# Where layer 1's two biases are added: bfloat16 products on TensorE, or adds on GpSimd and VectorE

## The chip, the cores and the metric

The kernel runs on one core of a Trainium2 chip. The metric is device time in microseconds (us). Before the change the median of three runs is 1116.52 us (1116.37 to 1117.14). One further execution was taken with the hardware profiler: it took 1114.53 us, of which 1112.8 us lie between its first and its last instruction (the span).

Five engines work beside each other, each through its own queue in order: PE (TensorE, matrix products and transposes; PEld is its weight load), DVE (VectorE), ACT (ScalarE), POOL (GpSimd) and SP (SyncE, which here issues the DMAs). POOL cannot read PSUM, the memory that PE writes to; DVE and ACT can.

## The reference, cut to what matters

Four graph layers run over x, 32 batches of 512 nodes with 128 features. Each layer normalises x, takes the positive part, applies its own function and adds the result to x. The change is in layer 1 alone:

```python
h = relu(layernorm(x))
# layer 1
h = h @ Wp + bp                               # 512 x 128
scores = h @ a_src [:, None] + h @ a_dst [None, :]
attn = softmax(where(adj <= 0, lowest, leaky(scores, 0.2)))
h_gat = relu(layernorm((attn * adj) @ h) * gat_g + gat_b)
h_gin = (1 + eps) * h_gat + adj @ h_gat
z = h_gin @ W1 + b1
z = relu(layernorm(z) * mlp_g + mlp_b)        # the inner norm
x = x + relu(z @ W2 + b2 + h_gat)
```

`bp` and `b1` are the two biases of the title. Both stand ahead of a layer norm over the features, so only their deviation from their own mean matters for the features: the kernel works with centred weights and centred biases. `bp` also moves the two scores of a node, by `bp . a_src` and `bp . a_dst`.

## The kernel before, in words

A batch is a tile of 128 partitions x 4 chunks x 128 features (512 nodes, four chunks of 128). All of x stays on the chip in `xs`. Nothing loops at run time: the program is unrolled, one chain of operations for every pair of layer and batch, 32 chains for each of the four layers, and two side chains, `prepare` (weights and biases, beside layer 0) and `prepare_last` (layer 3's attention matrix, beside layer 1).

The order on every engine is written out by a planner (`Plan.run`). Every `op(engine, length, emit, reads, writes)` gives it a length in us and the values that the operation reads and writes. It goes through a model of the five engines and always emits the operation that can begin first, among equals the one with the earliest due time. A chain's due times begin a gap after the chain before it (13.3 for layer 1) and at most 7 chains (`WINDOW`) are open at once. Buffers come from rooms of fixed size: 8 PSUM banks, 5 tiles written by DVE, 6 by ACT, 5 by POOL, 5 for the projected and scored `h`, 9 spare ones. What the planner emits first on an engine runs first there, whether or not it is ready.

Layer 1's chain (L793 to L856), the engine of each step in brackets:

- the outer norm: statistics [DVE L475, L477], negative mean [DVE L501], reciprocal deviation by a power [POOL L487, L489], `xn` [POOL L510, four instructions], transposes to `pt` [PE L386], relu to `hT` [ACT L519]
- the projection (`project_scored`), twice for two chunks each: a product of bfloat16 `ones3` with `b3_p` [PE L552, 128x260] opens the PSUM group, two float32 products [PE L557] add to it; then a copy to `h` [ACT L377]. Columns 0 to 127 are the features, column 128 the source score, column 129 the destination score
- the attention (`attend`): the destination scores are spread over all partitions by transposes to `prow` [PE L386]; `y = prow + mask` with its row maximum [DVE L587, four]; `top` and `nmax` [DVE L598, L602]; leaky relu with the source score as bias [ACT L612, four]; exponential with its sum [ACT L620, four]; transposes [PE L386]; `pT = pt * adjT` [DVE L629, four]; `po = pT' h` [PE L640]
- the norm of the attention's result: `q`, statistics of `po`, `ve` [DVE L802, L475, L806], power [POOL L815], `hn` [DVE L822, four], `+ gat_b` [POOL L827], relu to `hg` [ACT L829]
- `pg = hg' adjTe` [PE L834], copy to `ginT` [ACT L377], `hgb = hg + b2` [POOL L842]
- the inner layer: a product of `ones3` with `b3_1` [PE L530, 128x512] opens the group, then `pz` [PE L535]; statistics of `pz`, read in PSUM [DVE L475, L477]; power [POOL L487, L489]; `zn = pz * rz` [DVE L846]; transposes [PE L386]; `zT` with relu, gain and bias [ACT L850]; `px` [PE L535]; `res` and `xs` [DVE L854, L855]

The bfloat16 operands are made once in `prepare`: the centred bias is split into three bfloat16 terms, which lie in rows 0 to 2 of `b3_p` and `b3_1`, and `ones3` has ones in its first three rows, so that one bfloat16 product adds the bias at float32's precision to every node. The split takes DVE instructions (L972 to L992).

Of the kernel before, what the change touches and what calls it, by code (L numbers as in the profile page):

```python
# [229 lines left out]
def kernel(  # L230
# [52 lines left out]
    def const(name, shape, dtype=F32):  # L283
        return cp.tile(list(shape), dtype, name=name)
# [18 lines left out]
    def value(r, name):  # L303
        return Value(Slot(r, name))
# [50 lines left out]
    b3_p = const("b3_p", (P, P2), BF16)  # L355
    b3_1 = const("b3_1", (P, P), BF16)
    ones3 = const("ones3", (P, P), BF16)
# [8 lines left out]
    v_bias, v_w1, v_w2, v_wz, v_b3, v_adjTe, v_rows, v_mlp = (Value() for _ in range(8))  # L366
# [97 lines left out]
    def dve(length, emit, reads, writes):  # L464
        op(DVE, length, emit, reads, writes)
# [16 lines left out]
    def inv_dev(mv):  # L482
        rstd = Value()

        def emit():
            ve = small("ve")
            nc.gpsimd.tensor_scalar(ve, mv.own[:, :, 1], LN_EPS, 1.0, ALU.add, ALU.mult)  # L487
            rstd.own = small("rstd")
            nc.gpsimd.tensor_tensor(rstd.own, ve, mhalf, ALU.pow)  # L489

        op(POOL, 1.3, emit, [mv], [rstd])
        return rstd
# [29 lines left out]
    def column(hT, c):  # L522
        return hT.t[:, c, :]

    def project(hT, w, reads, b3=None, name="p"):
        pt = value(banks, name)

        def emit():
            if b3 is not None:
                nc.tensor.matmul(  # L530
                    pt.t, lhsT=ones3, rhs=b3.rearrange("p (o f) -> p o f", o=1).to_broadcast([P, C, P]),
                    start=True, stop=False,
                )
            for c in range(C):
                nc.tensor.matmul(  # L535
                    pt.t[:, c, :], lhsT=column(hT, c), rhs=w,
                    start=(b3 is None), stop=(b3 is None or c == C - 1),
                )

        op(PE, 0.9 + (0.22 if b3 is not None else 0.0), emit, [hT, *reads], [pt])  # L540
        return pt

    def project_scored(hT, w_ext, reads, b3=None):

        h = parts(scored, "h", 2)
        for k in range(2):
            pt = value(banks, "proj")

            def emit(k=k, pt=pt):
                p = pt.t.rearrange("p (c t) f -> p c (t f)", c=2)[:, :, 0:P2]  # L550
                if b3 is not None:
                    nc.tensor.matmul(  # L552
                        p, lhsT=ones3, rhs=b3.rearrange("p (o f) -> p o f", o=1).to_broadcast([P, 2, P2]),
                        start=True, stop=False,
                    )
                for c in range(2):
                    nc.tensor.matmul(  # L557
                        p[:, c, :], lhsT=column(hT, 2 * k + c), rhs=w_ext,
                        start=(b3 is None), stop=(b3 is None or c == 1),
                    )  # L560

            op(PE, 0.46 + (0.11 if b3 is not None else 0.0), emit, [hT, *reads], [pt])
            copy_op(
                ACT, 0.26, lambda k=k: h[k].t[:, 2 * k : 2 * k + 2, :],
                lambda pt=pt: pt.t.rearrange("p (c t) f -> p c (t f)", c=2)[:, :, 0:P2], [pt], [h[k]],
            )
        return h
# [7 lines left out]
    def attend(h, weights, v_weights):  # L575
# [19 lines left out]
        def emit_top():  # L595

            ntop.own = small("top")
            nc.vector.scalar_tensor_tensor(ntop.own, rmax.own, -1.0, h[0].t[:, :, P], ALU.mult, ALU.subtract)  # L598
# [5 lines left out]
        dve(0.08, emit_top, [*top, *h], [ntop])  # L604
# [3 lines left out]
        for ib in range(C):  # L608

            def emit_leaky(ib=ib):  # L610
                yw = wide(y[ib].t)
                nc.scalar.activation(yw, yw, AF.Prelu, alpha=0.2, bias=h[0].t[:, ib, P : P + 1])  # L612

            op(ACT, 0.61, emit_leaky, h, [y[ib]])
# [30 lines left out]
            op(PE, 0.9, emit_po, [pT, *h], [po[ib]])  # L645
# [147 lines left out]
    def layer1(b):  # L793
        hT, _ = preln(b)
        h = project_scored(hT, w1_ext, [v_w1, v_b3], b3_p)
        po, ssum = attend(h, adjT, v_adjT)
# [46 lines left out]
        pz = project(ginT, wz, [v_wz, v_b3], b3_1, "pz")  # L843
        rz = inv_dev(variances(lambda c: pz.t[:, c, :], [pz]))
        zn = value(by_dve, "zn")
        op(DVE, 0.6, lambda: nc.vector.tensor_mul(zn.t, pz.t, per_chunk(rz.own)), [pz, rz], [zn])  # L846
# [5 lines left out]
        px = project(zT, wts[:, W_2, :], [v_wts[W_2]], name="px")  # L852
# [6 lines left out]
    def layer2(b):  # L859
        hT, _ = preln(b)  # L860
        h = project_scored(hT, w2_ext, [v_w2])
        po, ssum = attend(h, None, None)
# [19 lines left out]
    def layer3(b):  # L882
# [7 lines left out]
        p1 = project(hT, wts[:, W_31, :], [v_wts[W_31]], name="p1")  # L890
# [21 lines left out]
    def prepare():  # L912
        wt_p, wt_1, wt_l2, row_p, row_1 = (value(spare, n) for n in ("wt_p", "wt_1", "wt_l2", "row_p", "row_1"))
# [13 lines left out]
        load(lambda: row_p.t[:, 0, :], all_rows(l1_bp), [row_p], 0.25)  # L927
        load(lambda: wt_1.t[:, 0, :], l1_w1, [wt_1], 0.25)
        load(lambda: row_1.t[:, 0, :], all_rows(l1_b1), [row_1], 0.25)
# [15 lines left out]
        def centred(dst, src, reads, writes):  # L945
# [8 lines left out]
        bp_c = value(spare, "bp_c")  # L954
        b1_c = value(spare, "b1_c")
        centred(lambda: w1_ext[:, 0:P], lambda: wt_p.t[:, 0, :], [wt_p], [v_w1])
        centred(lambda: wz, lambda: wt_1.t[:, 0, :], [wt_1], [v_wz])
        centred(lambda: wide(bp_c.t)[:, 0:P], lambda: row_p.t[:, 0, :], [row_p], [bp_c])
        centred(lambda: wide(b1_c.t)[:, 0:P], lambda: row_1.t[:, 0, :], [row_1], [b1_c])
# [4 lines left out]
        op(PE, 0.15, lambda: nc.tensor.matmul(  # L964
            pc1.t[:, 0, 0:2], lhsT=bp_rep.t[:, 0, :], rhs=a1[:, 0:2], start=True, stop=True), [bp_rep, v_a1], [pc1])
        copy_op(DVE, 0.1, lambda: wide(bp_c.t)[:, P:P2], lambda: pc1.t[:, 0, 0:2], [pc1], [bp_c])


        not0, not01, sel = (const(n, (P, 1)) for n in ("not0", "not01", "sel"))
        v_sel = Value()  # L970

        def selectors():  # L972
            nc.vector.tensor_scalar(not0, ident[:, 0:1], -1.0, 1.0, ALU.mult, ALU.add)
            nc.vector.tensor_sub(not01, not0, ident[:, 1:2])
            nc.vector.tensor_reduce(sel, ident[:, 0:3], AX.X, ALU.add)
            nc.vector.tensor_copy(ones3, sel.to_broadcast([P, P]))

        dve(0.5, selectors, [], [v_sel, v_b3])
        for src, out3, n in ((bp_c, b3_p, P2), (b1_c, b3_1, P)):
            tmp = value(spare, "terms")  # L980

            def terms(src=src, out3=out3, n=n, tmp=tmp):
                full = wide(src.t)[:, 0:n]
                kept = wide(tmp.t)[:, 0:P].bitcast(BF16)[:, 0:n]
                part = wide(tmp.t)[:, 2 * P : 2 * P + n]
                for drop in (not0, not01):
                    nc.vector.tensor_copy(kept, full)
                    nc.vector.tensor_scalar(part, kept, drop, None, ALU.mult)
                    nc.vector.tensor_sub(full, full, part)
                nc.vector.tensor_copy(out3, full)  # L990

            dve(1.2, terms, [v_sel], [src, tmp, v_b3])  # L992
# [256 lines left out]
```

## Time and profile before

| | busy us, whole span | share | busy us, 207 to 720 us (layer 1) |
|---|---|---|---|
| PE | 1085.5 | 98% | 505.31 of 513 |
| DVE | 922.5 | 83% | 452.25 of 513 |
| ACT | 672.1 | 60% | 316.57 of 513 |
| POOL | 673.2 | 60% | 279.96 of 513 |

The span is 1112.8 us, the profiled execution's own time 1114.53 us, the median of the unprofiled runs 1116.52 us. The granted TensorE clock is 0.994 over the span, 1.00 in every stretch from 40 us to 1080 us.

How to read it: busy is the union of an engine's instructions, each from its start to its end. Matmuls are pipelined, so one of 275 ns is followed by the next after about 110 ns; what a product costs is the distance to the next start, not its length. The stretch from 207 to 720 us begins with the first L552 (207.5 us) and ends with the last `xs` of layer 1 (718.3 us). It also holds the last chains of layer 0, the first of layer 2, and most of `prepare_last`.

### The profile page before, as it was taken

What the parts mean: (1) busy time and instruction counts of PE and PEld (TensorE: products, weight loads), DVE (VectorE), ACT (ScalarE), POOL (GpSimd) and SP (SyncE); (2) the same over time, 40 slices, a digit from 0 to 9 for tenths busy, and PEclk for the clock granted to TensorE, in tenths of its full rate; (3) what the DMA queues carried; (4) which work ended last, traced back from release to release, by engine and by line L of the source; (5) the groups of instructions that cost most, each with busy time, mean ns of one, the idle gap of its engine ahead of it and who ended that gap; (6) DMA issues with size and microseconds to landing.
All of it is one profiled execution on the core that took longest, in us unless ns stands there. A gap on an engine that the chain in (4) does not pass through costs nothing.

```text
span 1112.8 us, 25144 instructions
## 1 busy us (share of the span) xinstructions
PE 1085.5 (98%) x8680; PEld 989.0 (89%) x8683; DVE 922.5 (83%) x3822; ACT 672.1 (60%) x1588; POOL 673.2 (60%) x1040
## 2 busy tenths in 40 slices
PE   5999999999999999999999999899999999999998
PEld 4899999998787877887788887899999999999997
DVE  8989899978889898998989897977777777777772
ACT  3456455567365565574656765866667766766661
POOL 8355454554546555646456555687776777777773
PEclk8899999999999999999999999999999999999999
DMA  7202210000000000000000000000100000000001
GB/s 189 58 11 50 43 36 2 2 2 2 1 1 1 1 1 1 1 1 1 1 1 2 1 1 1 1 20 20 30 21 20 21 20 20 20 21 29 21 21 39
DMA packets 56911, 20.50 MB, mean 18 GB/s; under 512 B 21584, under 2 KB 56272, under 8 KB 56784
## 3 DMA queue, kind: packets, MB, share of 16 engines
q1 hardware_dynamic: 56784, 18.90, 6.9%
q8 instruction: 69, 1.13, 0.4%
q14 instruction: 58, 0.48, 0.1%
HBM read 10.43 MB, written 8.39 MB: 17 GB/s over the span
## 4 chain that ended last, share of the span: by engine, by line
PE 75%; DVE 16%; ACT 3%; POOL 2%; issue 1%; SPq 1%; DMA 1%; POOLq 0%; ACTq 0%; DVEq 0%
PE po L640 16%; PE pt L386 13%; PE po L784 10%; PE po L901 10%; PE proj L557 6%; PE pg L834 5%; DVE y L587 4%; PE prow L386 3%; PE po L776 2%; ACT y L620 2%; DVE st L475 2%; PE po L897 2%; PE p L535 2%; DVE pT L629 2%; PE pz L535 1%
## 5 line engine op out<-in xcount | busy, mean ns | idle before, releaser
L640 PE MATMUL po<-h,pT 128*128 128x128 f32 x2048 | 244.2, 275 | 1.7 <-DVE pT L379 1.0
L510 POOL TENSOR_SCALAR xn<-xs,nmean,rstd 128x128 f32<-128x128 f32 x512 | 232.0, 469 | 19.7 <-DVE st L475 9.6
L640 PEld LDWEIGHTS po<-h,pT 128*128 128x128 f32 x2048 | 236.3, 192 | 5.8 <-issue 1.9
L620 ACT ACTIVATE y<-y,nmax 128x512 f32<-128x512 f32 x256 | 181.7, 712 | 41.1 <-DVE nmean L501 20.1
L612 ACT ACTIVATE y<-y,h 128x512 f32<-128x512 f32 x256 | 165.4, 712 | 37.4 <-DVE rmax L587 37.1
L489 POOL TENSOR_TENSOR rstd<-ve,mhalf 128x4 f32<-128x4 f32 x160 | 163.9, 1024 | 13.4
L587 DVE CUSTOM_DVE_ANT_0 y<-prow,bias 128x512 f32<-128x512 f32 x256 | 161.9, 683 | 9.5 <-PE prow L386 9.0
L519 ACT ACTIVATE hT<-pt 128x512 f32<-128x512 f32 x128 | 75.5, 591 | 125.0 <-PE pt L386 123.2
L386 PE MATMUL pt<-ident,y 128*128 128x128 f32 x1024 | 135.1, 274 | 2.5 <-ACT y L620 1.8
L901 PE MATMUL po<-h,offT 128*128 128x128 f32 x1024 | 135.4, 275 | 0.5 <-ACT h L377 0.5
L487 POOL TENSOR_SCALAR ve<-mv 128x4 f32<-128x4 f32 x160 | 36.7, 229 | 160.9 <-DVE rsum L756 57.7
L386 PEld LDWEIGHTS pt<-ident,y 128*128 128x128 f32 x1024 | 115.7, 141 | 20.0 <-ACT y L620 11.4
L834 PE MATMUL pg<-adjTe,hg 128*128 128x512 f32 x256 | 128.2, 593 | 0.0
L901 PEld LDWEIGHTS po<-h,offT 128*128 128x128 f32 x1024 | 124.6, 192 | 0.6 <-ACT h L377 0.6
L475 DVE BATCH_NORM_STATS2 st<-xs 128x6 f32<-128x128 f32 x512 | 109.9, 276 | 1.5 <-POOL xs L879 1.4
L557 PE MATMUL proj<-w_ext,hT 128*128 128x130 f32 x768 | 107.8, 279 | 2.3 <-ACT hT L519 2.3
L557 PEld LDWEIGHTS proj<-w_ext,hT 128*128 128x128 f32 x768 | 97.7, 194 | 6.7 <-ACT hT L519 2.9
L377 ACT COPY h<-proj 128x260 f32<-128x260 f32 x192 | 67.6, 371 | 46.3 <-PE proj L557 40.5
L879 POOL TENSOR_TENSOR xs<-xs,em 128x512 f32<-128x512 f32 x32 | 40.9, 1278 | 81.2 <-DVE em L878 81.2
L386 PE MATMUL pt<-ident,xn 128*128 128x128 f32 x512 | 85.2, 279 | 2.7 <-POOL xn L510 1.9
L629 DVE TENSOR_TENSOR pT<-pt,adjT 128x512 f32<-128x512 f32 x128 | 82.1, 680 | 3.4 <-PE pt L386 3.2
L742 ACT ACTIVATE y<-y,nmax 128x256 f32<-128x256 f32 x128 | 63.8, 501 | 31.1 <-DVE rs L760 14.0
(189 smaller groups left out, 2101.2 us busy)
## 6 DMA issues: line engine op xcount, KB each, us to landing
xs<-in_x_dram SPq DMA_DIRECT2D x32, 256.0 KB, 3.6
out_dram<-yo SPq DMA_DIRECT2D x32, 256.0 KB, 2.2
u<-h SPq DMA_DIRECT2D x128, 0.5 KB, 1.8
bias<-in_adj_dram SPq DMA_DIRECT2D x4, 256.0 KB, 3.3
wts<-in_L_gnn_W_dram SPq DMA_DIRECT2D x3, 64.0 KB, 3.8
rows<-in_L_gnn_bias_dram SPq DMA_DIRECT2D x2, 64.0 KB, 3.3
wt_o<-L_gnn_others_weight_dram SPq DMA_DIRECT2D x1, 64.0 KB, 2.3
wts<-n_L_gnn_self_weight_dram SPq DMA_DIRECT2D x1, 64.0 KB, 3.8
```

Of the source, the lines that this page charges most:

```text
L386: nc.tensor.transpose(dst(k), src(k), ident)
L475: nc.vector.bn_stats(st[:, c, :], src(c))
L489: nc.gpsimd.tensor_tensor(rstd.own, ve, mhalf, ALU.pow)
L510: nc.gpsimd.tensor_scalar(xn.t[:, c, :], src[:, c, :], nmean.own[:, c : c + 1], rstd.own[:, c : c + 1], ALU.add, ALU.mult,)
L557: nc.tensor.matmul(p[:, c, :], lhsT=column(hT, 2 * k + c), rhs=w_ext, start=(b3 is None), stop=(b3 is None or c == 1),)
L587: nc.vector.tensor_tensor_reduce(wide(y[ib].t), wide(prow.t), bias[:, ib, :], 1.0, LOWEST, ALU.add, ALU.max, rmax.own[:, ib : ib + 1],)
L612: nc.scalar.activation(yw, yw, AF.Prelu, alpha=0.2, bias=h[0].t[:, ib, P : P + 1])
L620: nc.scalar.activation(yw, yw, AF.Exp, bias=nmax.own[:, ib : ib + 1], accum_out=ssum[0].own[:, ib : ib + 1])
L640: nc.tensor.matmul(po[ib].t[:, ib, :], lhsT=pT.t[:, jb, :], rhs=h[0].t[:, jb, 0:P], start=(jb == 0), stop=(jb == C - 1),)
L784: nc.tensor.matmul(po[ib].t[:, ib, :], lhsT=w, rhs=(hs if ib < H else hs2).t[:, jb, :], start=False, stop=(jb == C - 1),)
L834: nc.tensor.matmul(wide(pg.t), lhsT=hg.t[:, nb, :], rhs=adjTe[:, nb, :], start=(nb == 0), stop=(nb == C - 1))
L901: nc.tensor.matmul(po[ib].t[:, ib, :], lhsT=offT[:, jb, blk(ib)], rhs=h1.t[:, jb, :], start=False, stop=(jb == C - 1),)
```

## The change

The two bias products leave TensorE, with `b3_p`, `b3_1`, `ones3` and what made them. In their place:

- `src`, the source score with both score biases in it (`score_p`, one number in every partition), is made by a DVE instruction of 4 columns as soon as `h` is copied; `top` and the leaky relu read it instead of `h`'s column 128. A bias on the destination score and the same on the source score come to the same sum.
- the feature bias is added to `h`'s columns 0 to 127 in place by one POOL instruction, which only the products `po` wait for.
- `b1` is added to `pz` by DVE, from PSUM into `zn`; the statistics are then taken from `zn` in SBUF, and the scaling by `rz`, which was DVE's, is done by ACT in place, one instruction for each chunk.
- in `prepare` the centred biases are left as float32 rows, and one small product more adds the two score biases up.

```diff
-    b3_p = const("b3_p", (P, P2), BF16)
-    b3_1 = const("b3_1", (P, P), BF16)
-    ones3 = const("ones3", (P, P), BF16)
+    row_p = const("row_p", (P, 1, P))
+    row_1 = const("row_1", (P, 1, P))
+    score_p = const("score_p", (P, 1))
...
-    def project(hT, w, reads, b3=None, name="p"):
+    def project(hT, w, reads, name):
...
-            if b3 is not None:
-                nc.tensor.matmul(
-                    pt.t, lhsT=ones3, rhs=b3.rearrange("p (o f) -> p o f", o=1).to_broadcast([P, C, P]),
-                    start=True, stop=False,
-                )
...
-    def project_scored(hT, w_ext, reads, b3=None):
+    def project_scored(hT, w_ext, reads):
...
-                if b3 is not None:
-                    nc.tensor.matmul(
-                        p, lhsT=ones3, rhs=b3.rearrange("p (o f) -> p o f", o=1).to_broadcast([P, 2, P2]),
-                        start=True, stop=False,
-                    )
...
-    def attend(h, weights, v_weights):
+    def attend(h, src, v_src, v_h, weights, v_weights):
...
-            nc.vector.scalar_tensor_tensor(ntop.own, rmax.own, -1.0, h[0].t[:, :, P], ALU.mult, ALU.subtract)
+            nc.vector.scalar_tensor_tensor(ntop.own, rmax.own, -1.0, src(), ALU.mult, ALU.subtract)
...
-                nc.scalar.activation(yw, yw, AF.Prelu, alpha=0.2, bias=h[0].t[:, ib, P : P + 1])
+                nc.scalar.activation(yw, yw, AF.Prelu, alpha=0.2, bias=src()[:, ib : ib + 1])
...
-            op(PE, 0.9, emit_po, [pT, *h], [po[ib]])
+            op(PE, 0.9, emit_po, [pT, *v_h], [po[ib]])
...
-        h = project_scored(hT, w1_ext, [v_w1, v_b3], b3_p)
-        po, ssum = attend(h, adjT, v_adjT)
+        h = project_scored(hT, w1_ext, [v_w1])
+        src, v_h = Value(), Value()
+
+        def emit_src():
+            src.own = small("src")
+            nc.vector.tensor_scalar(src.own, h[0].t[:, :, P], score_p, None, ALU.add)
+
+        dve(0.08, emit_src, [*h, v_score_p], [src])
+        op(POOL, 1.25, lambda: nc.gpsimd.tensor_add(
+            h[0].t[:, :, 0:P], h[0].t[:, :, 0:P], row_p.to_broadcast([P, C, P])), [*h, v_row_p], [v_h])
+        po, ssum = attend(h, lambda: src.own, [src], [v_h], adjT, v_adjT)
...
-        pz = project(ginT, wz, [v_wz, v_b3], b3_1, "pz")
-        rz = inv_dev(variances(lambda c: pz.t[:, c, :], [pz]))
+        pz = project(ginT, wz, [v_wz], "pz")
         zn = value(by_dve, "zn")
-        op(DVE, 0.6, lambda: nc.vector.tensor_mul(zn.t, pz.t, per_chunk(rz.own)), [pz, rz], [zn])
+        op(DVE, 0.6, lambda: nc.vector.tensor_add(zn.t, pz.t, row_1.to_broadcast([P, C, P])), [pz, v_row_1], [zn])
+        rz = inv_dev(variances(lambda c: zn.t[:, c, :], [zn]))
+
+        def emit_zn():
+            for c in range(C):
+                nc.scalar.activation(zn.t[:, c, :], zn.t[:, c, :], AF.Copy, scale=rz.own[:, c : c + 1])
+
+        op(ACT, 0.88, emit_zn, [rz], [zn])
...
-        centred(lambda: wide(bp_c.t)[:, 0:P], lambda: row_p.t[:, 0, :], [row_p], [bp_c])
-        centred(lambda: wide(b1_c.t)[:, 0:P], lambda: row_1.t[:, 0, :], [row_1], [b1_c])
+        centred(lambda: row_p[:, 0, :], lambda: row_p[:, 0, :], [], [v_row_p])
+        centred(lambda: row_1[:, 0, :], lambda: row_1[:, 0, :], [], [v_row_1])
...
-        dve(0.5, selectors, [], [v_sel, v_b3])
-        for src, out3, n in ((bp_c, b3_p, P2), (b1_c, b3_1, P)):
-            tmp = value(spare, "terms")
...
-            dve(1.2, terms, [v_sel], [src, tmp, v_b3])
+
+        def emit_pc1():
+            for k in range(2):
+                nc.tensor.matmul(
+                    pc1.t[:, 0, 0:1], lhsT=bp_rep.t[:, 0, :], rhs=a1[:, k : k + 1], start=(k == 0), stop=(k == 1)
+                )
+
+        op(PE, 0.25, emit_pc1, [bp_rep, v_a1], [pc1])
+        copy_op(DVE, 0.1, lambda: score_p, lambda: pc1.t[:, 0, 0:1], [pc1], [v_score_p])
```

Layer 2 calls `attend` with the column of `h` in place of `src`, and so stays as it is. No DMA is added or taken away.

## The prediction

> **What bounds the kernel now.** I read the page first, then busy time by stage, the groups by form, and the timeline where a price hangs on a few instructions.
>
> ```profile
> span 1112.8 us, 25144 instructions
> PE 1085.5 (98%) x8680; PEld 989.0 (89%) x8683; DVE 922.5 (83%) x3822; ACT 672.1 (60%) x1588; POOL 673.2 (60%) x1040
> PE 75%; DVE 16%; ACT 3%; POOL 2%; issue 1%; SPq 1%; DMA 1%; POOLq 0%; ACTq 0%; DVEq 0%
> ```
>
> PE is busy in 98% of the span and carries 75% of the chain that ended last. The second line is busy time by engine, the third the chain by engine. By stage (layer 0 once it runs, layer 1, layers 2 and 3; columns PE, PEld, DVE, ACT, POOL, granted clock):
>
> ```profile
> 60.00:207.00 147.00, 147.00 (x1322) 146.81 (x1321) 134.74 (x747) 81.78 (x296) 72.76 (x142) 1.00 0.15 27
> 207.00:720.00 513.00, 505.31 (x3609) 419.34 (x3610) 452.25 (x1760) 316.57 (x690) 279.96 (x389) 1.00 0.00 1
> 720.00:1070.00 350.00, 349.91 (x3105) 344.21 (x3105) 263.50 (x965) 236.06 (x503) 262.61 (x408) 1.00 0.07 22
> ```
>
> The change works in the middle row. There PE is idle for only 7.7 us of 513, DVE is busy for 88%, ACT for 62%, POOL for 55%. The first row matters too: with DVE at 92% PE was never idle, so a DVE that full can still feed PE. The clock is 1.00, so no throttle enters the sum.
>
> **What is removed from PE.** Groups by form, then two stretches of the timeline (start, length):
>
> ```profile
> L552 PE MATMUL proj<-b_p,ones 128*128 128x260 bf16 x64 | 17.5, 274 | 0.0
> L530 PE MATMUL pz<-b,ones 128*128 128x512 bf16 x32 | 12.1, 379 | 0.0
> ```
> ```profile
> 386.36 0.27 PE L552 MATMUL proj<-b_p,ones 128*128 128x260 bf16 x1
> 386.47 0.61 PE L557 MATMUL proj<-w_ext,hT 128*128 128x130 f32 x4
> ```
> ```profile
> 508.44 0.38 PE L530 MATMUL pz<-b,ones 128*128 128x512 bf16 x1
> 508.66 1.05 PE L535 MATMUL pz<-wz,ginT 128*128 128x128 f32 x8
> ```
>
> The lengths (17.5 + 12.1 = 29.6 us) overstate the price, since matmuls are pipelined. From start to next start L552 holds PE for 0.11 us and L530 for 0.22 us: 64 x 0.11 + 32 x 0.22 = 7.0 + 7.0 = 14.0 us. Their weight loads lie beside other products. PE is the full engine here, so all of it counts: **-14.0 us**, if the other engines keep up.
>
> **`prepare`.** The splitting into three terms (14 DVE instructions, 29.45 to 33.65 us in the timeline) and the selectors go, some 5 us of DVE while it is full; two small products and nothing on SP's queue are added, since every load stays. After 29 us PE waits in that ramp for only about 2 us (0.69 at 38.9 and at 42.8 us, both for `hT`). Bounds 0 and -2; I take -1, half, as other DVE work moves up but the outer norms on POOL do not. The 3.7 us that PE stands before L964 stay: `bp_rep` still follows the centring.
>
> **DVE.** `zn`'s add reads PSUM as its product did (L846, 680 ns): no difference. Statistics from SBUF cost what they cost from PSUM (276 and 279 ns, medians of L475). New is `src`, 32 times a 128x4 scalar instruction like L501 (median 165 ns; 0.07 to 0.15 to the next start): 32 x 0.11 = 3.5 us of DVE. The 8.9 us that DVE stood idle before L846 for POOL's `rstd` leave DVE's queue: ACT now waits for it. What counts more is this pair, and two groups:
>
> ```profile
> 254.62 1.26 POOL L827 TENSOR_TENSOR hn<-hn,rows 128x512 f32<-128x512 f32 x1 [4.43 <-DVE top L598]
> 254.64 1.26 DVE L602 SCALAR_TENSOR_TENSOR nmax<-top 128x4 f32<-128x4 f32 x1
> ```
> ```profile
> L602 DVE SCALAR_TENSOR_TENSOR nmax<-top 128x4 f32<-128x4 f32 x64 | 19.2, 301 | 0.4
> L827 POOL TENSOR_TENSOR hn<-hn,rows 128x512 f32<-128x512 f32 x32 | 40.7, 1272 | 45.4 <-DVE top L598 24.4 <-DVE hn L822 9.4 <-DVE nmax L602 7.3
> ```
>
> A 4-column DVE instruction whose median is 150 ns takes 1.26 us when it meets a whole-tile add on POOL: it ends with that add. Means less medians give the holds of this stage: L602 64 x 0.151 = 9.7, L802 32 x 0.063 = 2.0, L598 1.3, L855 1.1, together 14 us, under 82 us of POOL adds (L827, L842). A third add (32 x 1.27 = 41 us) makes these half as many again: +7 us. And `src` waits for the very copy of `h` that the new add waits for, so the two meet often. A hold of `src` lies between 0 (it always starts first) and 1.27 us (always just after): 0 to 41 us. I take 0.4 us, 13 us in all: POOL is busy 55% of the stage, so in about half the cases its add starts too late to catch `src`. DVE gains 3.5 + 7 + 13 = 24 us.
>
> How much reaches PE? At worst all of PE's 7.7 idle us came from 14 us of holds, a share of 0.55, and 20 new us give 11; at best they hide behind the work queued ahead of PE (0). Nearest is the row above: its hold of 1.1 us over the median left PE idle for 0.65 us (before `pt`, at 256.9, waiting for L620), but most holds left no such gap, and those of `src` come before the 2.4 us of L587 and are partly made up. I take 0.3: **+6 us**.
>
> The Trainium skill (SBUF — State Buffer, "Who interferes with whom") says that VectorE and GpSimd share a port pair as an exclusive lock, held for a whole instruction, and counts scalar operations on SBUF among those that can want it. By it every late `src` is held to the end of the add, which is the upper end above and rival B; were `src` exempt, DVE would gain 11 us instead of 24. Another page (GPSIMD Engine Reference, "Engine selection") sends elementwise adds to VectorE, as GpSimd is about twice as slow; the trace has 1272 ns against 680. By that rule the bias add would be 19 us more of DVE and no lock.
>
> **POOL.** The 41 us raise it from 55% to 64% of the stage. Behind the add in POOL's queue stand the powers and outer norms of other batches (L489, L815, L510), later by up to 1.27 us; DVE's `hn` waits for one of them (7.5 us in all, at L822). `po` needs the add only after L587, both activations and the transposes, over 5 us later. The add touches columns 0 to 127 and `prow` reads column 129 of the same tile; that such accesses are not serialised is shown early on, where DVE reads columns 0 to 255 of each chunk of `adjT` while ACT writes others between them:
>
> ```profile
> 8.41 0.98 DVE L451 TENSOR_SCALAR biasT<-adjT 128x256 f32<-128x256 f32 x4
> 8.53 0.59 ACT L377 COPY adjT<-pt_adj 128x512 f32<-128x512 f32 x1 [0.27 <-PE pt_adj L386]
> ```
>
> **ACT.** New are 128 scalings of 128x128.
>
> ```profile
> L620 ACT ACTIVATE y<-y,nmax 128x512 f32<-128x512 f32 x256 | 181.7, 712 | 41.1 <-DVE nmean L501 20.1 <-DVE nmax L602 17.2 <-DVE ve L806 3.3
> L742 ACT ACTIVATE y<-y,nmax 128x256 f32<-128x256 f32 x128 | 63.8, 501 | 31.1 <-DVE rs L760 14.0 <-DVE nmean L501 13.4 <-DVE nmax L715 3.5
> ```
>
> 512 and 256 columns give 0.82 ns a column, so about 0.40 us for 128; followers overlap by 0.10 (four L612 in 2.55 us), so 0.30 each: 128 x 0.30 = 38 us, ACT from 62% to about 71%. Behind them in ACT's queue stand exponentials, which PE waits for: PEld waits 11.4 us in all for L620 (34 times), the largest wait of PE on another engine. If each batch's scalings delayed one exponential by their wait, that wait would grow by up to half, 6 us; at best 0. I take **+2 us**. The longer way of `zn` itself costs nothing: PE comes to `zn`'s transposes well after `zn` is there (first `zn` at 275.6, first transposes at 287.1 us); if that cover went, 1.3 us a batch would show, 42 us at worst.
>
> **Sum.** -14.0 - 1 + 6 + 2 = -7.0 us, from the profiled execution's own 1114.53 us (span 1112.8, 1.7 around it): 1107.5. The median of the runs shown, 1116.52, lies 2.0 above that execution, so 1109.5 us, -0.6%.
>
> **Rivals.** About 0.2% (2.2 us) is what a measurement of this kernel can tell from no change.
> - A. PE's relief comes through whole, as PE is backlogged: -14.0 to -16 with `prepare`, 1100.5 to 1102.5. For it: layer 0 at 92% DVE. Against: the holds.
> - B. DVE becomes layer 1's bound, through `src` held by the new add. DVE then needs 452 + 3.5 + 7 + 32h us; if it can be busy 94% of the time (it reached 92% in layer 0 with PE as the bound), the stage takes (462.5 + 32h) / 0.94. That is 506 us at h = 0.4, and from h = 0.6 on it is over today's 513: slower. At h = 0.8 it is 519, +6, 1122.5; at 1.27 it is 535, +22, 1138. For it: the pair above, and that both start from one release. Against: DVE always has other work queued, which scatters their starts.
> - C. The gain is eaten exactly: holds at the 0.55 share (+11) and ACT at +3, so nothing is left: 1115.5.
> - D. ACT or POOL is late for everything: the new wait for `rz` in ACT's queue delays the exponentials by 1 us a batch, 32 us for a gain of 15: 1133. Against: both keep about 30% idle.
>
> **How the numbers follow.** Forecast 0.45 (its own range 1103 to 1114), A 0.10, C 0.10, B 0.28, D 0.07. So faster 0.55, same 0.10, slower 0.35. The range goes from A's 1100.5 to 1131, short of B's far end and most of D.
>
> **What would show it.** PE's busy time falls by 13 to 15 us in layer 1 while its idle time there rises by less than 10: forecast. Length of `src`: a mean of 0.5 us confirms my hold, 0.2 none, over 1 rival B. L602's mean above 0.35 us shows the holds grown. If DVE is over 95% busy in layer 1 and waits of PE for L629's `pT` or for L620 grow past 20 us, DVE or ACT has become the bound and the prediction is wrong; equally if PE's order in layer 1, which the planner writes anew, leaves it idle for reasons that no row here shows.

## The result, and the profile after

The changed kernel takes 1133.56 us (median of four runs, 1131.91 to 1134.19); the kernel before, run beside it, 1116.44 us. The ratio is 1.015, with an interval of 1.0132 to 1.0168: slower by 17 us, where the forecast was 1109.5 us and the range ended at 1131. The profiled execution took 1134.19 us, its span is 1132.5 us.

The page's first lines, and the chain that ended last by engine:

```profile
span 1132.5 us, 25163 instructions
PE 1088.4 (96%) x8589; PEld 987.9 (87%) x8589; DVE 931.1 (82%) x3836; ACT 702.9 (62%) x1716; POOL 714.0 (63%) x1072
PE 56%; DVE 31%; ACT 8%; POOL 2%; issue 1%; DMA 1%; SPq 0%; ACTq 0%; DVEq 0%; POOLq 0%
```

PE's share of the chain fell from 75% to 56%, and DVE's rose from 16% to 31%: a larger part of that chain now runs through DVE. PE is busy for longer than before (1088.4 us against 1085.5) though 96 products are gone. One reason is that it ran at half its clock for part of the time. Busy time by stage shows where (columns: length, PE, PEld, DVE, ACT, POOL, granted clock, DMA share, GB/s):

```profile
60.00:207.00 147.00, 146.82 (x1300) 146.03 (x1300) 135.94 (x752) 80.15 (x289) 71.95 (x138) 0.99 0.14 27
207.00:720.00 513.00, 500.05 (x3524) 411.01 (x3523) 466.20 (x1784) 354.69 (x826) 320.25 (x426) 1.00 0.01 1
720.00:1070.00 350.00, 338.46 (x2931) 332.14 (x2930) 249.30 (x930) 218.88 (x477) 251.14 (x391) 0.97 0.07 20
...
700.00:760.00 60.00, 46.35 (x308) 40.62 (x307) 35.62 (x142) 28.68 (x63) 40.10 (x66) 0.80 0.03 9
```

In the row of layer 1, PE's idle time rose only from 7.7 to 13.0 us. ACT has 38 us more work there and POOL 40 us, both almost as forecast. The loss shows below it. In the 60 us from 700 to 760, the passage from layer 1 to layers 2 and 3, PE is busy for 46 us at a clock of 0.80. The same window of the kernel before, one row of the same view:

```profile
700.00:760.00 60.00, 58.56 (x514) 57.11 (x514) 50.75 (x182) 43.06 (x94) 43.84 (x68) 1.00 0.05 15
```

PE issued 514 matmuls in those 60 us before and 308 after. To put a number on it, I added up, stretch by stretch, what each matmul's distance to the next start exceeds the usual distance of its form. Before, this lost time is 3.1 us between 700 and 760 us; after, it is 26.1 us. That is 23 us of new loss in one place. In the rest of layer 1 (207 to 700 us) it goes from 15.4 to 22.4 us, 7 us more.

### The passage

The timeline of after from the last batch's `zn` on, at the end of layer 1 (start, length, engine, line, operation; in brackets the engine's idle time before and what ended it):

```profile
701.20 0.69 DVE L838 TENSOR_TENSOR zn<-pz,row 128x512 f32<-128x512 f32 x1
...
703.58 0.83 DVE L475 BATCH_NORM_STATS2 st<-zn 128x6 f32<-128x128 f32 x4
...
709.02 1.01 POOL L489 TENSOR_TENSOR rstd<-ve,mhalf 128x4 f32<-128x4 f32 x1
...
714.25 2.54 ACT L596 ACTIVATE y<-y,h 128x512 f32<-128x512 f32 x4
...
719.76 0.71 ACT L604 ACTIVATE y<-y,nmax 128x512 f32<-128x512 f32 x1
...
720.47 1.27 ACT L843 ACTIVATE zn<-zn,rstd 128x128 f32<-128x128 f32 x4
...
728.99 0.60 PE L386 MATMUL pt<-ident,zn 128*128 128x128 f32 x4
...
730.46 1.16 PE L530 MATMUL px<-wts,zT 128*128 128x128 f32 x8 [0.87 <-ACT zT L849]
...
733.01 1.78 DVE L854 SCALAR_TENSOR_TENSOR xs<-res,xs 128x512 f32<-128x512 f32 x1
...
734.72 0.86 DVE L475 BATCH_NORM_STATS2 st<-xs 128x6 f32<-128x128 f32 x4
...
739.18 1.77 PE L386 MATMUL pt<-ident,xn 128*128 128x128 f32 x4 [7.56 <-POOL xn L510]
```

Read it downwards. `zn` is there at 701.9, its statistics end at 704.7, and the last power that can belong to them ends at 710.0. The scaling, which the change gave to ACT, starts only at 720.47: ahead of it in ACT's queue stand the leaky relus and exponentials of layer 2's batches. After it the transposes wait from 721.74 to 728.99, in which time PE works off products that its own queue has ahead of them. Then the rest of the chain (transposes, `zT`, `px`, `xs`) takes until 734.8. Only then does DVE begin the statistics of the next chains, one chain after another; they stand behind this one in DVE's queue, which fits the planner's limit of seven open chains. PE has nothing for 7.56 us. From 2 us into the wait on the granted clock, read in steps of 2 us, is 0.50 from 734 to 754 us.

The same steps of the kernel before:

```profile
701.86 0.69 DVE L846 TENSOR_TENSOR zn<-pz,rstd 128x512 f32<-128x512 f32 x1
...
703.96 0.80 ACT L850 ACTIVATE zT<-pt,mlp_gb 128x512 f32<-128x512 f32 x1
...
707.67 1.05 PE L535 MATMUL px<-wts,zT 128*128 128x128 f32 x8
...
718.34 0.69 DVE L855 SCALAR_TENSOR_TENSOR xs<-res,xs 128x512 f32<-128x512 f32 x1
718.95 0.86 DVE L475 BATCH_NORM_STATS2 st<-xs 128x6 f32<-128x128 f32 x4
```

From the start of `zn` to that of `xs` it was 16.5 us before; after, it is 31.8 us.

### `src` and the new add

Groups by form (columns: busy in all, mean ns of one, idle time before them and its releaser):

```profile
L843 ACT ACTIVATE zn<-zn,rstd 128x128 f32<-128x128 f32 x128 | 40.8, 392 | 17.2 <-POOL rstd L489 16.8
...
L787 POOL TENSOR_TENSOR h<-h,row_p 128x512 f32<-128x512 f32 x32 | 38.3, 1198 | 15.5 <-ACT h L377 15.5
...
L586 DVE SCALAR_TENSOR_TENSOR nmax<-top 128x4 f32<-128x4 f32 x64 | 18.4, 288 | 1.2
L784 DVE TENSOR_SCALAR src<-h,score_p 128x4 f32<-128x4 f32 x32 | 17.6, 549 | 3.9 <-ACT h L377 3.9
```

The mean of `src`, 549 ns, is the 0.5 us that the prediction named as the sign of its hold. (A hold is the time for which a DVE instruction takes longer because a POOL instruction is running.) A pair from the timeline:

```profile
240.05 1.24 DVE L784 TENSOR_SCALAR src<-h,score_p 128x4 f32<-128x4 f32 x1
240.09 1.18 POOL L787 TENSOR_TENSOR h<-h,row_p 128x512 f32<-128x512 f32 x1
```

In 14 of the 32 batches `src` ends 25 to 28 ns after the new add; where it meets no POOL instruction that holds it, it takes about 0.22 us. Below, "holds" are worked out from the trace in one way for all kernels: for every form of DVE instruction that stands at least five times in the trace, the time over the lower quartile of its lengths, where that is more than 0.04 us, summed from 207 to 720 us. Before they are 14.8 us, after 27.4 us, and 10.4 of these are `src`'s. The sum asks for no cause, but most of it is POOL's doing: 13.5 of the 14.8 us and 23.1 of the 27.4 us belong to instructions that end within 35 ns after a POOL instruction.

### The profile page after: what moved, and what is told of

Its sections match the earlier page's. It is cut to its first block, busy times and chain, and to the rows that moved or that the text cites. A ratio compares the mean times of both kernels' runs of the same rounds, so it can differ in the third digit from the quotient of the medians.

```text
span 1132.5 us, 25163 instructions
## 1 busy us (share of the span) xinstructions
PE 1088.4 (96%) x8589; PEld 987.9 (87%) x8589; DVE 931.1 (82%) x3836; ACT 702.9 (62%) x1716; POOL 714.0 (63%) x1072
## 4 chain that ended last, share of the span: by engine, by line
PE 56%; DVE 31%; ACT 8%; POOL 2%; issue 1%; DMA 1%; SPq 0%; ACTq 0%; DVEq 0%; POOLq 0%
PE po L624 10%; PE po L768 9%; PE po L900 9%; PE pt L386 7%; DVE st L475 6%; PE proj L544 6%; PE pg L827 5%; DVE y L571 4%; DVE pT L613 4%; ACT y L604 3%; DVE pT L379 2%; PE po L760 2%; PE po L896 2%; DVE mv L477 2%; PE prow L386 2%; ACT y L596 2%
## 5 line engine op out<-in xcount | busy, mean ns | idle before, releaser
L624 PE MATMUL po<-h,pT 128*128 128x128 f32 x2048 | 247.8, 277 | 2.5 <-ACT num L1145 0.7
L604 ACT ACTIVATE y<-y,nmax 128x512 f32<-128x512 f32 x256 | 181.7, 712 | 18.5 <-DVE nmax L586 13.5
L487 POOL TENSOR_SCALAR ve<-mv 128x4 f32<-128x4 f32 x160 | 34.7, 217 | 142.5 <-DVE rsum L740 42.8
L596 ACT ACTIVATE y<-y,h 128x512 f32<-128x512 f32 x128 | 82.4, 711 | 56.3 <-DVE rmax L571 55.0
L596 ACT ACTIVATE y<-y,src 128x512 f32<-128x512 f32 x128 | 82.7, 712 | 32.1 <-DVE rmax L571 31.0
L386 PE MATMUL pt<-ident,xn 128*128 128x128 f32 x512 | 83.8, 281 | 11.8 <-POOL xn L510 10.4
```

Source lines behind the costliest of these rows:

```text
L386: nc.tensor.transpose(dst(k), src(k), ident)
L596: nc.scalar.activation(yw, yw, AF.Prelu, alpha=0.2, bias=src()[:, ib : ib + 1])
L604: nc.scalar.activation(yw, yw, AF.Exp, bias=nmax.own[:, ib : ib + 1], accum_out=ssum[0].own[:, ib : ib + 1])
L624: nc.tensor.matmul(po[ib].t[:, ib, :], lhsT=pT.t[:, jb, :], rhs=h[0].t[:, jb, 0:P], start=(jb == 0), stop=(jb == C - 1),)
```

## The experiments

Two things are thus new at the same time: a hole at the passage, and longer holds. Three theories went into the first four runs. O: the planner's new order, hole included, costs the time. H: the holds do. S: the scalings on ACT, which delay the exponentials, do. Each table row below is a run, "earlier" stands for the kernel after with the three last batches due earlier; the column "wait" is PE's longest wait for an `xn` of POOL in the whole trace, which is 1.7 us before and 7.6 us after.

| run | time, us | ratio to before | holds, us | wait, us |
|---|---|---|---|---|
| after | 1133.56 | 1.0150 [1.0132, 1.0168] | 27.4 | 7.6 |
| after, three last batches earlier | 1116.69 | 0.9999 [0.9986, 1.0012] | 29.1 | 1.5 |
| before, three last batches earlier | 1128.68 | 1.0101 [1.0081, 1.0122] | 11.6 | 4.6 |
| only `b1` changed | 1118.32 | 1.0011 [0.9995, 1.0026] | 18.3 | 0.4 |
| only `bp` changed | 1135.68 | 1.0161 [1.0136, 1.0186] | 30.7 | 7.4 |
| earlier, `src` from PSUM | 1104.91 | 0.9887 [0.9871, 0.9904] | 17.0 | 1.6 |
| earlier, no `src` | 1104.42 | 0.9882 [0.9867, 0.9897] | 19.9 | 1.5 |
| earlier, scaling on DVE | 1119.77 | 1.0027 [1.0013, 1.0041] | 31.5 | 1.4 |
| earlier, no `src`, scaling on DVE | 1106.33 | 0.9904 [0.9889, 0.9919] | 22.3 | 1.6 |
| after, short add | 1121.10 | 1.0054 [1.0033, 1.0076] | 16.3 | 7.5 |
| earlier, short add | 1106.90 | 0.9922 [0.9901, 0.9943] | 17.3 | 1.9 |
| after, `src` from PSUM | 1125.57 | 1.0086 [1.0060, 1.0113] | 17.9 | 7.5 |
| before, `hgb` added twice | 1124.48 | 1.0084 [1.0062, 1.0106] | 19.2 | 1.9 |

The kernel before took 1115.03 to 1117.88 us beside the different groups of runs, so kernels of different groups are compared by their ratios, times 1116.5 us.

### The order alone

Only due times are changed: the chains of layer 1's three last batches count as due 80 us earlier, so that the planner lets their tails go first. The same two lines go into the kernel after and into the kernel before.

```diff
         plan.chain(gap * RAMP if n < AHEAD else gap, name=layer.__name__)
+        if layer is layer1 and b >= B - 3:
+            plan.chains[-1][2] -= 80
```

> The changed kernel, with one thing more: the planner is told that the chains of layer 1's last three batches begin 80 us earlier, so that their last operations come before layer 2's in its order. No operation is added or left out. Theory O (order): the time lost is the hole at the passage from layer 1 to layer 2 (PE lost 26 us between 700 and 760 us, 3 us before the change), because the last batch's tail is planned late and the window of seven chains then shuts out new work. The hole goes and the time falls from 1133.6 to 1109 to 1116 us. Theory H (holds): DVE, held by POOL's new adds all through layer 1, is the loss and the hole is only where it comes to light; the time stays over 1125. Theory S (scaling): the new scalings in ACT's queue delay the exponentials all through layer 1; over 1125 as well.

> The kernel before, with the same 80 us for the last three chains of layer 1, as the control of that edit. Theory O: order alone, at the same work, moves the time by as much as the change did its gain: a hole of 5 to 12 us opens between 680 and 760 us, 1119 to 1129 us; it would mean that the order before was a lucky one. Theories H and S: no instruction is added and no hold, so the time stays within 3 us of 1116.4.

In the kernel after, the edit takes away the hole and 17 us (a ratio of 0.9999 where it was 1.0150); 1116.7 us is just above the 1109 to 1116 of theory O, and far from the 1125 and more of H and S. The window from 700 to 760 us, and from the view of waits PE's for an `xn` (us in all, times, longest):

```profile
700.00:760.00 60.00, 59.06 (x519) 57.65 (x517) 49.02 (x172) 42.49 (x94) 46.58 (x66) 1.00 0.05 14
```
```profile
PE pt L386 <- POOL xn L510: 1.5, 1, 1.5
```

PE issues 519 matmuls there at full clock, as the kernel before did. In the kernel before, the same edit does the reverse. It opens a hole with a wait of 4.6 us, and the kernel is 1.0% slower with the same operations (1128.7 us, inside O's 1119 to 1129), as the same two views show:

```profile
700.00:760.00 60.00, 52.29 (x418) 49.13 (x417) 44.09 (x168) 36.61 (x79) 45.20 (x70) 0.91 0.03 10
```
```profile
PE pt L386 <- POOL xn L510: 5.2, 3, 4.6
```

So the written order alone decides about 1 to 1.5% here, and one setting of due times suits one set of lengths and not the other. But without the hole the change was only as fast as the kernel before, not 7 us faster. Within layer 1 PE still lost 29.8 us (207 to 700 us, reckoned as above), against 15.4 before. That remainder needed a cause of its own. Part of it is the new order itself: without the earlier due times the kernel after lost 22.4 us there.

### One half of the change alone

In the first kernel `b1` is added by DVE and the scaling goes to ACT, while `bp` stays a bfloat16 product; in the second it is the other way round.

```diff
 # only b1
-        pz = project(ginT, wz, [v_wz, v_b3], b3_1, "pz")
-        rz = inv_dev(variances(lambda c: pz.t[:, c, :], [pz]))
+        pz = project(ginT, wz, [v_wz], None, "pz")
...
-        op(DVE, 0.6, lambda: nc.vector.tensor_mul(zn.t, pz.t, per_chunk(rz.own)), [pz, rz], [zn])
+        op(DVE, 0.6, lambda: nc.vector.tensor_add(zn.t, pz.t, row_1.to_broadcast([P, C, P])), [pz, v_row_1], [zn])
+        rz = inv_dev(variances(lambda c: zn.t[:, c, :], [zn]))
...
+        op(ACT, 0.88, emit_zn, [rz], [zn])
...
 # only bp
-        h = project_scored(hT, w1_ext, [v_w1, v_b3], b3_p)
+        h = project_scored(hT, w1_ext, [v_w1])
...
+        dve(0.08, emit_src, [*h, v_score_p], [src])
```

> Only the inner bias is changed: its product goes, DVE adds it, ACT does the scaling; bp stays a bfloat16 product. PE loses 6.9 us of work, ACT gains 38 us in layer 1, POOL nothing. S: slower, 1122 or more. H: faster, 1108 to 1112, as POOL has no new add. O: layer 1 up to 690 us takes 3 to 7 us less than before the change, and the total is this plus or minus what the passage to layer 2 loses, which the trace shows: 1110 to 1120.

> Only the projection's bias is changed: POOL adds it to h, DVE makes src; the inner bias stays a bfloat16 product and the scaling stays on DVE. PE loses 7.2 us of work, POOL gains 41 us, DVE the holds. H: slower, 1125 or more. S: faster, 1108 to 1112. O: layer 1 up to 690 us is no slower than before the change, and the total is set by the hole at the passage: 1115 to 1135, with the loss between 680 and 760 us.

Neither gains anything, though each removes 7 us of PE's work. With `b1` alone the time stays within what can be told from no change, with 3.5 us more of holds; PE lost 7.2 us between 700 and 720 us (before: 2.8). With `bp` alone both troubles are there: a wait of 7.4 us at the passage, and 30.7 us of holds, 17.2 of them at `src`. H had put the first of these runs lower and S higher than it came; in the second H's "1125 or more" came and S's 1108 to 1112 did not. O's spans held in the first and were overstepped by 0.7 us in the second, but as each half got an order of its own, these two runs could not part O from H.

### `src` out of the add's way

These two kernels, and the next two, keep the earlier due times, so that the hole is gone. `src` is made from PSUM, half a batch at a time, or it is not made at all: ACT's copy of the projection adds half of the score bias to all columns, and the bias row has it taken off.

```diff
 # src from PSUM
-            nc.vector.tensor_scalar(src.own, h[0].t[:, :, P], score_p, None, ALU.add)
...
+                nc.vector.tensor_scalar(src.own[:, 2 * k : 2 * k + 2], p[:, :, P], score_p, None, ALU.add)
...
 # no src
+                    nc.scalar.activation(h[k].t[:, 2 * k : 2 * k + 2, :], p, AF.Identity, bias=half)
...
+            nc.vector.tensor_scalar(score_p, pc1.t[:, 0, 0:1], 0.5, None, ALU.mult)
+            nc.vector.tensor_scalar(row_p[:, 0, :], row_p[:, 0, :], score_p, None, ALU.subtract)
```

> The kernel after with the three last batches of layer 1 planned 80 us earlier, and with src made from PSUM, two instructions of 128x2 a batch, one behind each half of the projection, in place of one of 128x4 from SBUF. Reference: the kernel after with the earlier batches alone, 1116.7 us, in which src took 17.5 us (mean 547 ns) and PE's stalls in layer 1 were some 13 us more than in the kernel before. Theory H (DVE held by GpSimd's adds is what eats PE's gain): src is no longer held if its source is not in SBUF, mean under 0.2 us, DVE gains 8 to 10 us back, of which PE gets about half: 1110 to 1113. Theory S (ACT's new scalings delay the exponentials, holds are hidden): 1115 to 1118. Theory P (the written order's own chance): anywhere from 1112 to 1122, with the difference lying in the passage to layer 2 and not spread over layer 1.

> The kernel after with the three last batches planned 80 us earlier and without src: half of the scores' constant is added to every column by ACT's copy of the projection (a bias of the copy), and taken from the bias row again in the preparation. Removes 32 DVE instructions, 17.5 us of DVE with their holds. H: DVE 17 us shorter, PE gets about half: 1107 to 1111, and less than the form with src from PSUM. S: 1114 to 1118, since ACT has as much to do. P: 1112 to 1122.

1104.91 and 1104.42 us: 12 to 13 us less than with the held `src`, and 1.1 to 1.2% less than the kernel before. The group of the first kernel shows that there are now twice as many instructions, and none is held (the longest takes 220 ns), although 11 of the 64 begin while a whole-tile add is running on POOL that goes on for over 0.1 us after they have ended:

```profile
L788 DVE TENSOR_SCALAR src<-proj,score_p 128x2 f32<-128x2 f32 x64 | 13.1, 206 | 3.9 <-ACT h L377 2.9 <-PE proj L544 0.9
```

DVE spends 13.1 us on them, only 4.4 us less than on the 32 held ones (17.5 us in the kernel with the earlier batches). Yet the time falls by 12.5 us, about as much as the holds (29.1 to 17.0 us). Leaving `src` out altogether takes those 13 us off DVE as well and brings only 0.5 us more, within the spread of the runs; DVE's other holds were 2.9 us longer there. This speaks for being held, and not being busy, as what cost the time. H had expected half of this gain.

### The scaling on ACT or on DVE

```diff
-        op(ACT, 0.88, emit_zn, [rz], [zn])
+        op(DVE, 0.6, lambda: nc.vector.tensor_mul(zn.t, zn.t, per_chunk(rz.own)), [rz], [zn])
```

> The kernel after with the three last batches planned 80 us earlier and the scaling of zn on DVE again (one 128x512 product in place, from SBUF), so ACT loses 128 instructions (41 us) and DVE gains 32 of about 0.7 us (22 us) plus what GpSimd's adds hold of them. S: the exponentials are no longer late, 1106 to 1111. H: DVE is the fuller engine, it becomes the bound in layer 1: 1122 to 1130. P: 1112 to 1122.

> Both: no src, and the scaling of zn on DVE. H: the scaling costs DVE 22 us and the missing src gives back 17: 1116 to 1120, above the form that only leaves out src. S: 1105 to 1110, about the same as with the scaling on DVE alone. P: 1112 to 1122, in no order with the others.

S falls as the main cause: with the scaling on DVE the kernel is slower, by 3.1 us with `src` and by 1.9 us without. (The second time, 1106.3 us, lies in S's range, but S had the scaling's move bring a gain; the first, 1119.8 us, lies in the range of P alone, which is theory P of the expectations, the written order's own chance.) So ACT is the better place for the scaling, by little. It is the other half of the lesson that counts: 32 more whole-tile products on DVE (752 ns each), which the planner knew of, changed the time by only 2 to 3 us, and the holds rose by 2.4 us with them (29.1 to 31.5, 19.9 to 22.3 us). That is a net figure, since 41 us left ACT at the same time. H's price for DVE's work itself, 5 us and more, was too high.

### The holds with the order kept

The kernels with another `src` also had another order. In the next two nothing moves: the new add covers 4 columns of each chunk instead of 128 (the kernel leaves out the bias of the other 124), while the planner still counts it at full length.

```diff
-            h[0].t[:, :, 0:P], h[0].t[:, :, 0:P], row_p.to_broadcast([P, C, P])), [*h, v_row_p], [v_h])
+            h[0].t[:, :, 0:4], h[0].t[:, :, 0:4], row_p[:, :, 0:4].to_broadcast([P, C, 4])), [*h, v_row_p], [v_h])
```

> The kernel after with GpSimd's new add of the bias over 4 columns of each chunk instead of 128 (the bias of the other columns is left out of the result); every instruction, its place and the written order are those of the kernel after, hole at the passage to layer 2 included. Theory H1 (so far: every us that DVE is held unplanned in layer 1 costs PE about a us): holds of DVE in layer 1 fall from 27 to about 15 us, time falls by 10 to 13 us from 1133.6, to 1120.5 to 1123.5; the hole of some 20 us after 700 us stays. Rival W (what was priced before: 0.3 of a hold reaches PE): 1128 to 1131. Rival O1 (only the order matters, the gains seen with src from PSUM came from its new order): 1132 to 1135.

> The same short add in the kernel with the three last batches of layer 1 planned 80 us earlier, whose order is kept (1116.7 us with the whole add). H1: holds fall from 29 to about 15 us, 1103 to 1106, like the forms with src from PSUM or without src. W: 1111 to 1114. O1: 1115 to 1118.

> The kernel after with src made from PSUM, and no batch planned earlier, so that the planned hole at the passage to layer 2 is there again (a hole of 13 us in PE's own plan, as in the kernel after). If the two costs add up: 1133.6 less the 11.8 us that this edit gave in the other order, 1119 to 1124. If the hole hides the holds: 1128 to 1134. If the edit heals the hole too: 1104 to 1110.

In the order of the kernel after, the short add saves 11 us (ratio 1.0150 to 1.0054) and the holds fall by 11.1 us; the hole stays, with its wait of 7.5 us. In the other order it saves 8.6 us, for 11.8 us of holds; its 1106.9 us are just above H1's 1103 to 1106. The price of 0.3 of a hold (1128 to 1131 us in the first) is excluded, and so is the order as the source of this gain. The groups of the first kernel show the cause:

```profile
L784 DVE TENSOR_SCALAR src<-h,score_p 128x4 f32<-128x4 f32 x32 | 8.5, 267 | 3.9 <-ACT h L377 3.9
...
L787 POOL TENSOR_TENSOR h<-h,row_p 128x16 f32<-128x16 f32 x32 | 7.4, 230 | 18.5 <-ACT h L377 18.5
```

The same 32 instructions take 267 ns instead of 549 when the add beside them takes 230 ns instead of 1198.

The short add also takes 31 us of work off POOL, which would be a rival cause: whatever waits for POOL could start sooner. The waits do not show it. From 207 to 720 us the waits that POOL ended are 5.7 us of DVE after and 5.6 with the short add, and 42.8 and 42.7 us of ACT. What shrinks is PE's wait for the exponentials, here in the kernel before, the kernel after and the one with the short add (us in all, times, longest, from 207 to 720 us):

```profile
PEld pt L386 <- ACT y L620: 11.4, 34, 1.1
...
PEld pt L386 <- ACT y L604: 16.1, 34, 1.7
...
PEld pt L386 <- ACT y L604: 10.1, 29, 1.0
```

The third kernel still has all of ACT's scalings, so it is not they that made the exponentials late. PE's lost time from 205 us to the start of the last batch's `zn` says the same: 14.7 us before, 23.4 after, 14.6 with the short add (here with one usual distance for all kernels, taken over their traces, which gives slightly less than above). In the 60 us behind that `zn`, the passage, the loss stays (25.8 us after, 24.0 with the short add).

Making `src` from PSUM in the kernel after, with no other due times, gives 1.0086: 7 us less, for 9.5 us of holds, and the hole stays (23.0 us lost in the same 60 us). Its 1125.6 us lie between the two ranges, 1119 to 1124 for costs that add up and 1128 to 1134 for a hole that hides the holds. So both costs are there at once, but they do not simply add: the same edit was worth 12.5 us in the other order.

### A hold somewhere else

In the kernel before, POOL adds `hgb` twice in a row, so that DVE can be caught at instructions other than `src`; the written order is that of before.

```diff
-        op(POOL, 1.25, lambda: nc.gpsimd.tensor_add(hgb.t, hg.t, row_of(B_2)), [hg, v_rows], [hgb])
+        def emit_hgb():
+            for _ in range(2):
+                nc.gpsimd.tensor_add(hgb.t, hg.t, row_of(B_2))
+        op(POOL, 1.25, emit_hgb, [hg, v_rows], [hgb])
```

> The kernel before, with its whole-tile add on GpSimd that makes hgb issued twice in a row in layer 1 (same result, same written order, PE as before), so that DVE can be held by 32 more adds, at other instructions than src. H1: holds rise from 15 us by 4 to 10 us, and the time by as much: 1120 to 1127. Rival T (only a hold of src, at the head of the attention, costs; other holds are covered): 1116 to 1118.5.

The holds rise by 4.4 us and the time by 9.4 us. The 1116 to 1118.5 us of the theory that only a hold of `src` costs time did not come. But the time rose by twice the holds, and not all of it can be theirs: POOL also has 42 us more to do here, PE's waits for POOL's `xn` go from 1.9 to 4.4 us in all, and the trace has 3.4 us at half clock at 320 us that the kernel before has not. How much of the time is due to holds at other instructions is therefore not shown.

## Why the prediction was wrong, step by step

**The step that failed: nothing was priced at the passage to layer 2.** The prediction costed `zn`'s longer way at nothing, because PE came to `zn`'s transposes 11.5 us after `zn` had begun. That was read from the first batch. In the last batch the cover was gone: behind it come chains whose start waits for its end. The bound given, 1.3 us a batch, left out the queue, in which the scaling stood 10 us behind the exponentials of layer 2. More broadly, the prediction took the order around the change as given and named only in its last sentence that the planner writes it anew. With the hole healed by due times alone, the kernel is 17 us faster; the mirror run, where the same due times open a hole in the kernel before, shows that the place is sensitive whatever the biases do. That the scaling's position in ACT's queue alone made the hole is not shown: the kernel in which only `bp` moves has a hole as well, and its scaling is DVE's.

**The term that was mis-sized: how much of a hold reaches PE.** Priced at 0.3 of each us, with 0.55 as the worst. Measured between pairs of kernels:

| pair | holds, us | time, us |
|---|---|---|
| earlier: `src` from PSUM | -12.1 | -12.5 |
| earlier: short add | -11.8 | -8.6 |
| after: short add | -11.1 | -10.7 |
| after: `src` from PSUM | -9.5 | -7.1 |

That is 0.7 to 1.0, but each time is a difference of two medians and uncertain by 2 to 3 us. The two pairs with the short add can be compared more finely, as they have the same instructions in the same order: at 205 us, before layer 1, the kernel with the short add is already 2.5 us ahead (2.6 in the other pair; the traces with the whole add have 3.4 us at half clock at 85 us, the others have not), at 680 us 11.3 us (11.6). So 8.8 and 9.0 us come off in layer 1, for 11.1 and 11.8 us of holds: 0.8 of each us. The upper bound of 0.55 had been taken from the kernel before as all of PE's visible idle time over all holds. But PE can lose time without showing as idle, since a matmul's recorded length reaches over the start of the next, so the bound was too low.

**How the gap divides.** The forecast was 1109.5 us and 1133.6 were measured, 24 us more. By the lost time in the traces of before and after, 23 us of this lie at the passage. In layer 1 the loss grew by 7 us, and the sum had set 8 there (+6 for the holds, +2 for ACT). That this came so near is luck: the sum had 20 us of new holds at 0.3 each, and it came to 12.6 us at about 0.8, which is 10 instead of 6 (lost time and this price agree only to within 3 us); and ACT's +2 does not show, as the waits for the exponentials above say. The same edit of due times was worth 17 us in the kernel after, 15 with the short add and 22 with `src` from PSUM, and not 23, in part because it moved some loss into layer 1.

**What was right.**
- The mechanism of the hold, its place, and its size: 549 ns against the 0.5 us named, held in 14 of 32 batches ("about half"), 10.4 us in all against the 13 set. The mean hold of `src` is thus 0.33 us, where 0.4 was set. The holds at other instructions rose by 2.2 us, not 7; `nmax` itself fell (301 to 288 ns). The Trainium skill, in SBUF — State Buffer ("Who interferes with whom"), calls the shared ports an exclusive lock, held for a whole instruction; the 14 that end 25 to 28 ns after the add agree. In VectorE: DVE Perf Modes ("Why PSUM operands drop a tier") it says that an operand in PSUM shuts out the modes that need both read ports to SBUF; `src` from PSUM was not held once, not even in the 11 cases under a running add, which agrees as well.
- PE's relief. 14.0 us were set. Each matmul counted at the usual distance of its form, PE's work falls by 13.0 us, from 1065.4 to 1052.4 us. In the kernel after none of this reaches the total; in the one without `src` and without the hole, which is 13.2 us faster than before (0.9882), it does, together with what `prepare` saves. The sign named for it, PE's busy time in layer 1 down by 13 to 15 us, did not come: it fell by 5.3 us, as held-up products show as busy.
- The work of ACT (38 us set, 38 us more in layer 1) and of POOL (41 set, 40 measured). The shares given with them, 71% and 64%, are about 69% and 63% by the prediction's own rows (355 and 321 of 513 us), which is what was measured (69% and 62%).
- `prepare`: PE's lost time in the first 60 us went from 21.6 to 19.4 us, where -1 was set, with -2 as the bound. In the profiled execution the 3.4 us at half clock at 85 us took it back: from 60 to 207 us the loss rose by 2.0 us.

**The rivals.** B came nearest in mechanism (`src` held by the add), but not in reason: DVE did not run out of time, for it was busy 91% of the stage, and over 20 us more of known work on it cost 2 to 3 us net. (Its threshold is h = 0.62 rather than 0.6: at 0.6 its formula gives 512 us.) D came nearest in time, 1133 us, but it was the other way round: it let exponentials wait behind a scaling, 1 us in each batch; in the trace one scaling waits behind the exponentials, for 10 us, in the last batch.

## What to carry to other kernels

Where the order on the engines is written out ahead, a change of lengths rewrites it everywhere: look at the seams between stages, where the next stage can wait for the last chain, and price the last batch by itself, not by the first. Give the new lengths a new setting of due times before judging the change; here that alone was worth 1.5%, as much as all that was changed.

Work that the planner knew of was cheap here on an engine that is 90% full (13 us of it more or less moved the time by 0.5 us), while each us for which the same engine was held up unplanned cost about 0.8 us. So first move a small instruction out of the way of a long one on the other engine: here a source in PSUM, or a constant carried by a copy that runs anyway, took the kernel with the earlier due times from no change to 1.1 and 1.2% faster.

## What the runs showed of the hardware

- A DVE instruction whose record starts before the add's can still be held by it: at 240.05 us `src` starts 37 ns ahead of the add and ends 27 ns after it. That happened in three batches, 37 to 44 ns ahead each; the three that started about 0.1 us or more ahead (98, 117 and 424 ns) were not held to the new add's end.
- The same operation with its input in PSUM, on two columns instead of four, was never held, in 64 cases (median 209 ns, at most 220 ns); 11 of these ran under a whole-tile add of POOL.
- Around PE's 7.56 us of waiting the granted clock was at one half for 20 us (734 to 754 us), 15 of them with PE at work again. In the kernel with the short add, whose wait at the same place is 7.5 us, it was half for 10 us. The wait so cost more than itself here: 23 us more than before were lost at the passage.
